# Transposes two groups ahead in a graph network's edge loop, with a new order of copy, softplus and bias

## The chip, the core and the metric

The kernel runs on one core of a Trainium2 chip, as one launch. The metric is the device time of a run in microseconds (us). The time before is the median of nine runs. One further execution was recorded by the hardware profiler; all durations below come from that one.

## What is computed

A layer of a graph network: 12500 nodes with 64 features, 200000 edges sorted by their destination, with 64 features each. Cut to what matters (`ssp(x) = softplus(x) - log 2`):

```python
nodes = node_state[edges].reshape(num_edges, -1)            # source and destination rows, 128 wide
gates = ssp(edge_state @ We1 + be1) @ We2 + be2
soft_cutoff = 1.0 - jax.nn.sigmoid(5.0 * (edges_distance - (CUTOFF - 1.5)))
gates = gates * soft_cutoff
h = ssp(nodes @ Wn1 + bn1) @ Wn2 + bn2
messages = h * gates
message_sum = jnp.zeros_like(node_state).at[edges[:, 1]].add(messages)
new_state = node_state + (ssp(message_sum @ Ws1 + bs1) @ Ws2 + bs2)
x = layernorm(x + new_state)
```

## The kernel before

The edges are cut into 391 groups of 512 (NG = 391, so `last` = 390). A group is four columns of 128 edges. For each group the kernel does the following, each on the engine named, in float32:

- **gather** (GpSimd, L233): an indirect DMA per column brings 128 rows of x, one per edge, into the tile `xg`. There are 19 buffers of `xg` (AHEAD + BEHIND), and the gathers of group i+14 are issued in step i. A few columns (26 in all) are not gathered but fetched as single rows by ScalarE's DMA queue into `xr` (`fetch`, L259, up to nine rows in a step). ROWS = (0, 9) gives the rows per step of SyncE's queue and of ScalarE's.
- **load** (SyncE, L280 and L288): the group's edge features `eT` and a window of 42 rows of a table that holds the destination's part of the first layer, into `wns`. Queued five steps ahead (LOADS).
- **onehot** (VectorE, L295): writes beside each gathered row which of 42 destinations of the window it belongs to. Both of its inputs are in SBUF.
- **transposes** (TensorE, L309; L306 for single rows): four transposes put features and one-hots on the partitions, in the PSUM tile `tx`, of which there are two buffers. Here the step waits for its gathers, loads and one-hot.
- **xcopy** (ScalarE, L316): `tx` to the SBUF tile `xT`.
- **layer 1** (TensorE): the bias (L321), the edge features (L326) and the node rows (L332) into the PSUM tile `z`, of which there are two buffers.
- **exps, logs** (ScalarE, L343 and L346) and **softplus** (VectorE, L351): the first nonlinearity, from `z` over `u` to `s`.
- **layer 2** (TensorE): the bias (L356), the gates (L363) and h (L368) into the PSUM tile `gh`.
- **hcut, message** (VectorE, L377 and L381): h times the cutoff, times the gates, to `msg`.
- **scatter** (TensorE, L385): `msg` times the one-hots, into a corner of the `z` tile of a later group.
- **window** (VectorE, L402): adds that corner to `sums` at the window's place.

In a step i of the loop TensorE works on layer 1 of group i+1, on layer 2 of group i and on an older group's scatter. `behind_by` says whose: group i-2 until the close, which begins at step 378 (`last - CLOSE`, CLOSE = 12); in step 378 both i-2 and i-1; after that i-1. The last two groups are written out behind the loop.

Whenever the groups that can reach a block of nodes are done, that block's own network and norm are put into the steps that follow (`node_block`, `parts`). Their TensorE parts (`hidden`, L421, and `layer2`, L449 and L452) use a `tx` tile and stand between `layer2(i)` and the end of the step. `hidden` reads `sums`, so it waits for the last window before it. In step 378 there is one such `hidden`.

The order of each engine's queue is the order of the program (`manual_schedule`): no scheduler moves anything. Each engine runs its queue in order, so what waits holds up what stands behind it on the same engine. GpSimd has only gathers in the loop.

Of the kernel before, what the change touches and what calls it, by code (L numbers as in the profile page):

```python
# [71 lines left out]
CLOSE = 12  # L72
# [53 lines left out]
def gnn_resnorm_kernel(ctx: ExitStack, tc: tile.TileContext, a: dict, out: bass.AP, E: int):  # L126
# [23 lines left out]
    def gh_tile():  # L150
        return psum.tile([P, NB], F32, name="gh")

    def tx_tile():
        return psum.tile([P, NB], F32, name="tx")
# [15 lines left out]
    packed, at = {}, 0  # L170
# [21 lines left out]
    def note(key, ins):  # L192
        made.setdefault(key, []).append(ins)
        return ins
# [19 lines left out]
    def arrived(g, k):  # L214
        n = by_rows[g, k]
        queue = slots[n][0]
        n -= firsts[queue]
        return landed[queue][n % LANDED], 16 * P * (n // LANDED + 1)
# [18 lines left out]
    def rows_left(queue):  # L237
        return (firsts[queue + 1] - firsts[queue]) * P - fetched[queue]
# [12 lines left out]
    def fetch(i, queue, count):  # L251

        for _ in range(min(count, rows_left(queue)) if i >= ROWS_FROM else 0):
            n, r = divmod(fetched[queue], P)
            n += firsts[queue]
            _, g, k = slots[n]
            if r == 0:
                row_tiles[n, "in"], xrs[g, k] = row_tile(queue, n), row_tile(queue, n)
            ins = queues[queue].dma_start(row_tiles[n, "in"][r : r + 1, :D].bitcast(U8),  # L259
                                          x_bytes[:, bass.ds(row_at[queue].pop(0), 4 * D)])  # L260
            tc.no_tile_sem_insts.add(ins.ins.name)
            ins.then_inc(arrived(g, k)[0], 16)
            if r == 0:
                behind(ins, ("rows read", n - 2))
            fetched[queue] += 1
# [3 lines left out]
    def row_tile(queue, n):  # L269
        return nc.alloc_sbuf_tensor_at(f"xr{queue}_{n % 2}", [P, P], F32,  # L270
                                       offset=rows_base + (2 * queue + n % 2) * 4 * P).ap()
# [30 lines left out]
    def transposes(g, *needs):  # L302
        tx = tx_tile()[:DW].rearrange("f (k e) -> f k e", k=K)
        for k in range(K):
            if (g, k) in by_rows:
                ins = nc.tensor.transpose(tx[:, k, :], xrs[g, k][:, :DW], ident)  # L306
                note(("rows read", by_rows[g, k]), ins.wait_op(*arrived(g, k), "sem-ge"))
            else:
                ins = nc.tensor.transpose(tx[:, k, :], xgs[g][:, k, :DW], ident)  # L309
            if k == 0:  # L310
                behind(ins, *needs)
        xTs[g] = tx

    def xcopy(g):
        xT = work.tile([DW, K, P], F32, name="xT", bufs=3)
        note(("xcopy", g), nc.scalar.copy(xT, xTs[g]))  # L316
        xTs[g] = xT.rearrange("f (t h) e -> f h t e", h=2)
# [17 lines left out]
    def z_of(g):  # L335
        return zs[g].rearrange("p b e -> p (b e)")[:, : 3 * HE]
# [11 lines left out]
    def softplus(g, part=every):  # L348
        if part.start == 0:
            ss[g] = work.tile([P, 3, 2, P], F32, name="s", bufs=3)  # L350
        nc.vector.scalar_tensor_tensor(ss[g].rearrange("p i t e -> p (i t e)")[:, part], us[g][:, part], BIG,  # L351
                                       z_of(g)[:, part], OP.min, OP.max)

    def layer2_bias(g):
        gh = gh_tile()
        nc.tensor.matmul(gh, ones3[:, :P], row3.rearrange("q i k d -> q (i k d)"), start=True, stop=False,  # L356
                         skip_group_check=True)
        ghs[g] = gh.rearrange("p (i k d) -> p i k d", i=2, k=K)
# [38 lines left out]
    def window(g):  # L397
        if g not in window_at:
            window_bases(g)
        for h in range(2):  # L400
            part = sums[h * D : (h + 1) * D, bass.ds(window_at[g][h], W)]
            nc.vector.tensor_add(part, part, scs[g][h * D : (h + 1) * D, h * W : (h + 1) * W])  # L402
# [89 lines left out]
    with tc.manual_schedule():  # L492
# [124 lines left out]
        with tc.tile_pool(name="finish", bufs=1) as finish:  # L617
            blocks = list(zip(node_blocks(N), block_steps(N, NG)))
            last = NG - 1
            parts, begun, complete, rest = {}, None, 0, []  # L620

            def at(f, g, *more):
                if 0 <= g < NG:
                    f(g, *more)

            def behind_by(i):
                close = last - CLOSE
                return [g for g in ([i - 2] if i <= close else []) + ([i - 1] if i >= close else []) if g >= 0]

            for g in range(LOADS - 1):  # L630
                load(g)
            for g in range(2):
                onehot(g)
            for i in range(-1, last - 1):
                now = parts.pop(i, [])
                early = [part for part in now if part.tensor]
                at(load, i + LOADS)
                if i >= 0:
                    at(gather, i + AHEAD)
                transposes(i + 1, ("load", i + 1), ("gather", i + 1), ("onehot", i + 1))  # L640
                xcopy(i + 1)
                read_rows(i, 1, ROWS[1])
                fetch(i, 1, ROWS[1] - 6)
                layer1_bias(i + 1)
                at(layer2_bias, i)
                for n, g in enumerate(behind_by(i)):
                    scatter(g, zs[i + 1][:, 1, HE + 2 * n * W : HE + 2 * (n + 1) * W])
                layer1_edge(i + 1)
                layer1_node(i + 1)
                exps(i + 1)  # L650
                fetch(i, 1, 3)
                logs(i + 1)
                fetch(i, 1, 3)
                for g in behind_by(i):
                    window(g)
                at(layer2, i)
                for part in early:
                    part.tensor(tx_tile())
                at(hcut, i)
                at(message, i)  # L660
                softplus(i + 1)
                for part in early:
                    part.others()
                at(onehot, i + 3)
                for part in now:
                    if not part.tensor:
                        part.others()
                complete = i
                if blocks and complete >= blocks[0][1] - PREPARE and not begun:
                    begun = node_block(*blocks[0][0], finish)  # L670
                    begun.pop(0).others()
                if blocks and complete >= blocks[0][1]:
                    steps = next(steps for steps in BLOCK_STEPS if i + steps[-1] < last - 1)
                    for n, part in zip(steps, begun):
                        parts.setdefault(i + n, []).append(part)
                    rest = begun[len(steps) :]
                    blocks.pop(0)
                    begun = None
            assert len(blocks) == 1 and begun and not parts


            begun.pop(2).others()
            transposes(last, ("load", last), ("gather", last), ("onehot", last))
            xcopy(last)
            layer1_bias(last)
            layer2_bias(last - 1)
            scatter(last - 2, zs[last][:, 1, HE : HE + 2 * W])
            layer1_edge(last)
            layer1_node(last)
            for some in (edge, node):  # L690
                exps(last, some)
                logs(last, some)
            square, variance, root, scale, store = (part.others for part in rest)
            square()
            window(last - 2)
            for g in range(last - 1, last + 1):
                window_bases(g)
            layer2(last - 1)
            layer2_bias(last)
            softplus(last, edge)  # L700
            layer2_edge(last)
            softplus(last, node)
            layer2_node(last)
            hcut(last - 1)
            message(last - 1)
            scatter(last - 1, tx_tile()[:, : 2 * W])
            variance()
            root()
            hcut(last)
            message(last)  # L710
            scatter(last, tx_tile()[:, : 2 * W])
            window(last - 1)
            window(last)
            hidden, clamp = begun.pop(0)
            hidden(gh_tile())
            scale()
            clamp()
            store()
            for part in begun:
                node_part(part)  # L720
# [154 lines left out]
```

## Time and profile before

| | before |
|---|---|
| median of 9 runs | 1960.89 us (1959.08 to 1963.64) |
| the profiled execution's own time | 1961.36 us |
| its span in the profile | 1959.4 us |
| TensorE matmuls (PE) | 1791.6 us busy, 91% of the span |
| TensorE weight loads (PEld) | 1467.0 us, 75% |
| VectorE (DVE) | 1048.8 us, 54% |
| ScalarE (ACT) | 964.4 us, 49% |
| GpSimd (POOL) | 1460.8 us, 75% |
| granted TensorE clock, mean | 0.971 |

A row of the groups shows line, engine, operation, output and inputs, and how often; then the busy time and the mean of one in ns; then the idle time of the engine just before these instructions and what ended most of it. A row of the timeline shows start and duration in us, and in square brackets the idle time before it and its releaser, where there was any. Matmuls are pipelined, so the busy time of one reaches into the next. A row of the chain of waits shows start and duration of the piece of work, or the wait, that set what came next. A row by stretches of time shows for each engine its busy time and number of instructions, in the order PE, PEld, DVE, ACT, POOL, and then the granted clock, the DMA share and GB/s.

### The profile page before, as it was taken

The numbers are of one execution on the slowest core, as the hardware profiler recorded it, in microseconds if no ns is written. First come the engines' busy times: TensorE is split into PE (matmuls) and PEld (weight loads), VectorE is DVE, ScalarE is ACT, GpSimd is POOL, SyncE is SP. The second block draws the span as 40 slices with busy tenths as digits, with TensorE's granted clock in tenths as the row PEclk, the third lists the DMA queues.
The fourth block names the chain that finished last, engine by engine and source line by source line (L and its number), as shares of the span: only waits on it lengthen the run. The fifth ranks groups of instructions, "written<-read, shape, count | busy, mean of one in ns | idle before, by whom it ended". The sixth has DMA issues, their size and how long they took to land.

```text
span 1959.4 us, 42161 instructions
## 1 busy us (share of the span) xinstructions
PE 1791.6 (91%) x11373; PEld 1467.0 (75%) x11373; DVE 1048.8 (54%) x2746; ACT 964.4 (49%) x1318; POOL 1460.8 (75%) x1541
## 2 busy tenths in 40 slices
PE   4899999999889989998989989998989999999997
PEld 4787777787777777777777777787777777777775
DVE  4355555555544545555555555555555555465555
ACT  1355555555444544444444444555455555455543
POOL 7777777777777777777777777777777777777773
PEclk9999999999999999999999998989999999899998
DMA  8423332332223232322232222332222232233221
GB/s 244 138 70 71 71 72 65 72 70 67 64 66 67 64 69 64 69 64 69 64 69 66 67 69 65 69 69 67 69 69 67 69 69 69 62 78 71 68 66 26
DMA packets 146162, 143.14 MB, mean 73 GB/s; under 512 B 46847, under 2 KB 93355, under 8 KB 145922
## 3 DMA queue, kind: packets, MB, share of 16 engines
q1 hardware_dynamic: 88714, 87.55, 15.5%
q0 software_dynamic: 49184, 50.46, 14.5%
q10 hardware_dynamic: 8024, 2.37, 0.6%
q8 instruction: 97, 1.59, 0.3%
q14 instruction: 143, 1.17, 0.2%
HBM read 130.58 MB, written 9.63 MB: 72 GB/s over the span
## 4 chain that ended last, share of the span: by engine, by line
PE 49%; ACTq 20%; issue 9%; ACT 8%; DMA 6%; DVE 4%; POOL 1%; SPq 1%; DVEq 0%; POOLq 0%
ACTq L259 17%; PE z L332 10%; PE gh L368 7%; PE z L385 7%; PE tx L309 7%; PE z L326 5%; ACT xT L316 4%; PE gh L363 4%; ACTq L247 3%; DMA xg<-in_x,src_i 3%; ACT u L343 3%; PE gh L356 2%; PE z L321 2%; DVE h L377 2%; PE z L593 2%
## 5 line engine op out<-in xcount | busy, mean ns | idle before, releaser
L233 POOL DMA_INDIRECT xg<-in_x,src_i x1537 | 1460.6, 950 | 471.4 <-issue 339.3
L343 ACT ACTIVATE u<-z 128x768 f32<-128x768 f32 x392 | 317.3, 809 | 703.5 <-PE z L332 687.7
L402 DVE TENSOR_TENSOR sums<-sums,z 64x42 f32 x778 | 152.9, 197 | 799.9 <-ACT u L343 770.9
L332 PE MATMUL z<-xT,wns 106*128 106x256 f32 x1564 | 427.3, 397 | 8.1 <-ACT xT L316 7.4
L368 PE MATMUL gh<-consts,s 128*128 128x64 f32 x3128 | 399.3, 271 | 0.0
L346 ACT ACTIVATE u<-u,one 128x768 f32<-128x768 f32 x392 | 366.0, 934 | 67.2 <-ACT u L343 64.2
L368 PEld LDWEIGHTS gh<-consts,s 128*128 128x128 f32 x3128 | 388.9, 195 | 0.1
L351 DVE SCALAR_TENSOR_TENSOR s<-u,z 128x768 f32<-128x768 f32 x392 | 369.2, 942 | 12.2 <-ACT u L346 10.0
L332 PEld LDWEIGHTS z<-xT,wns 106*128 106x128 f32 x1564 | 299.3, 197 | 78.1 <-ACT xT L316 31.4
L309 PE MATMUL tx<-consts,xg 128*106 128x128 f32 x1538 | 241.3, 278 | 111.5 <-DVE msg L381 31.5
L385 PEld LDWEIGHTS z<-xg,msg 128*128 128x128 f32 x1556 | 207.4, 194 | 127.2 <-issue 122.6
L316 ACT COPY xT<-tx 106x512 f32<-106x512 f32 x391 | 228.1, 583 | 147.0 <-PE tx L309 138.6
L309 PEld LDWEIGHTS tx<-consts,xg 128*106 128x106 f32 x1538 | 170.6, 139 | 133.4 <-issue 65.5
L385 PE MATMUL z<-xg,msg 128*128 128x84 f32 x1556 | 268.0, 295 | 1.2 <-DVE msg L381 0.6
L363 PEld LDWEIGHTS gh<-consts,s 128*128 128x128 f32 x1564 | 245.6, 198 | 25.2 <-DVE s L351 2.0
L326 PE MATMUL z<-eT,consts 128*128 128x256 f32 x782 | 256.9, 411 | 0.0
L363 PE MATMUL gh<-consts,s 128*128 128x128 f32 x1564 | 246.0, 280 | 1.7 <-DVE s L351 1.7
L377 DVE TENSOR_TENSOR h<-gh,cut 128x256 f32<-128x256 f32 x391 | 166.0, 424 | 31.6 <-PE gh L368 18.5
L381 DVE TENSOR_TENSOR msg<-gh,h 128x256 f32<-128x256 f32 x391 | 165.9, 424 | 13.4
L356 PE MATMUL gh<-row,ones 3*128 3x512 bf16 x391 | 148.4, 380 | 0.0
L295 DVE TENSOR_TENSOR xg<-consts,rel 128x168 f32<-128x168 f32 x391 | 128.3, 328 | 0.0
L326 PEld LDWEIGHTS z<-eT,consts 128*128 128x128 f32 x782 | 122.6, 198 | 1.2 <-issue 1.2
(93 smaller groups left out, 575.4 us busy)
## 6 DMA issues: line engine op xcount, KB each, us to landing
xr<-in_x ACTq DMA_DIRECT2D x3328, 0.2 KB
eT<-in_eT SPq DMA_DIRECT2D x195, 256.0 KB
xg<-in_x,src_i POOLq DMA_INDIRECT x1537
wns<-table SPq DMA_DIRECT2D x782, 21.0 KB
table<-tb SPq DMA_DIRECT2D x14, 448.0 KB
sums<-in_xT SPq DMA_DIRECT2D x7, 455.0 KB
y<-in_x SPq DMA_DIRECT2D x24, 128.0 KB
out<-y SPq DMA_DIRECT2D x24, 128.0 KB
```

What stands on the lines that cost most here:

```text
L233: note(("gather", g), nc.gpsimd.indirect_dma_start(out=xg[:, k, :D], out_offset=None, in_=x, in_offset=bass.IndirectOffsetOnAxis(ap=src_i[ ...
L259: ins = queues[queue].dma_start(row_tiles[n, "in"][r : r + 1, :D].bitcast(U8), x_bytes[:, bass.ds(row_at[queue].pop(0), 4 * D)])
L309: ins = nc.tensor.transpose(tx[:, k, :], xgs[g][:, k, :DW], ident)
L316: note(("xcopy", g), nc.scalar.copy(xT, xTs[g]))
L326: nc.tensor.matmul(zs[g][:, 0, :HE], we1.rearrange("a h d -> a (h d)"), eTs[g], start=False, stop=True, skip_group_check=True)
L332: nc.tensor.matmul(zn, wns[:, g % REST, h, :], xTs[g][:, h], start=True, stop=True, skip_group_check=True)
L343: nc.scalar.activation(us[g][:, part], z_of(g)[:, part], AF.Exp)
L346: nc.scalar.activation(us[g][:, part], us[g][:, part], AF.Ln, bias=one)
L351: nc.vector.scalar_tensor_tensor(ss[g].rearrange("p i t e -> p (i t e)")[:, part], us[g][:, part], BIG, z_of(g)[:, part], OP.min, OP.max)
L363: nc.tensor.matmul(v[:, 0, t], ss[g][:, 0, t, :], we2, start=False, stop=False, skip_group_check=True)
L368: nc.tensor.matmul(ghs[g][:, 1, 2 * t + h, :], ss[g][:, 1 + h, t, :], wn2, start=False, stop=h == 1 and t == 1, skip_group_check=True)
L385: ins = nc.tensor.matmul(sc, msgs[g][:, 2 * t : 2 * t + 2, :].rearrange("p h f -> p (h f)"), xgs[g][:, 2 * t : 2 * t + 2, D:DW], start=t = ...
```

## The change

The transposes run two groups ahead until the close: step i transposes group i+2 instead of i+1. Step -1 transposes groups 0 and 1, step 378 none, and the later steps i+1 as before. Until the close the copy of `tx` stands on ScalarE behind exps and logs of its step; the bias of layer 2 moves from the front of TensorE's step to just before layer 2; and softplus of group i+1 moves on VectorE ahead of `hcut` and `message` of group i. One-hots are made four groups ahead instead of three. Nothing is added to or taken from the work as a whole. In step 378 softplus already has its old place, and the bias still the new one.

```diff
+            def ahead_by(i):
+                return [0, 1] if i < 0 else [i + 2] if i < last - CLOSE else [i + 1] if i > last - CLOSE else []
+
             for g in range(LOADS - 1):
                 load(g)
-            for g in range(2):
+            for g in range(3):
                 onehot(g)
             for i in range(-1, last - 1):
...
-                transposes(i + 1, ("load", i + 1), ("gather", i + 1), ("onehot", i + 1))
-                xcopy(i + 1)
+                for g in ahead_by(i):
+                    transposes(g, ("load", g), ("gather", g), ("onehot", g))
+                    if i < 0 or i > last - CLOSE:
+                        xcopy(g)
                 read_rows(i, 1, ROWS[1])
                 fetch(i, 1, ROWS[1] - 6)
                 layer1_bias(i + 1)
-                at(layer2_bias, i)
+                if i > last - CLOSE:
+                    layer2_bias(i)
                 for n, g in enumerate(behind_by(i)):
                     scatter(g, zs[i + 1][:, 1, HE + 2 * n * W : HE + 2 * (n + 1) * W])
                 layer1_edge(i + 1)
...
                 logs(i + 1)
                 fetch(i, 1, 3)
+                if 0 <= i < last - CLOSE:
+                    xcopy(i + 2)
                 for g in behind_by(i):
                     window(g)
+                if 0 <= i <= last - CLOSE:
+                    layer2_bias(i)
                 at(layer2, i)
                 for part in early:
                     part.tensor(tx_tile())
+                if i < last - CLOSE:
+                    softplus(i + 1)
                 at(hcut, i)
                 at(message, i)
-                softplus(i + 1)
+                if i >= last - CLOSE:
+                    softplus(i + 1)
                 for part in early:
                     part.others()
-                at(onehot, i + 3)
+                at(onehot, i + 4)
```

## The prediction, made before the result was known

> **What bounds the kernel now.** I read the page's engine table and its group for the gathers first, then GpSimd alone near the end, then the chain of waits where the loop closes, then that place's timeline and clock.
>
> ```profile
> PE 1791.6 (91%) x11373; PEld 1467.0 (75%) x11373; DVE 1048.8 (54%) x2746; ACT 964.4 (49%) x1318; POOL 1460.8 (75%) x1541
> L233 POOL DMA_INDIRECT xg<-in_x,src_i x1537 | 1460.6, 950 | 471.4 <-issue 339.3
> ```
>
> TensorE shows 91%, but its group rows don't say whether it waits. GpSimd's row does: 1460.6 us busy and 471.4 idle over 1537 gathers is 0.307 us before each one. The timeline of GpSimd shows that this gap is always the same:
>
> ```profile
> 1927.68 1.07 POOL L233 DMA_INDIRECT xg<-in_x,src_i  x1 [0.30 <-issue]
> 1929.05 0.95 POOL L233 DMA_INDIRECT xg<-in_x,src_i  x1 [0.30 <-DMA xg<-in_x,src_i]
> 1930.30 0.94 POOL L233 DMA_INDIRECT xg<-in_x,src_i  x1 [0.30 <-DMA xg<-in_x,src_i]
> 1931.55 0.94 POOL L233 DMA_INDIRECT xg<-in_x,src_i  x1 [0.30 <-DMA xg<-in_x,src_i]
> ```
>
> A gather every 1.25 us, whoever is named as releaser: the gap belongs to the instruction, and GpSimd waited for nobody after its first index load (2.82 us). 1537 gathers from 3.29 to 1932.49 are 1929.2 us of the span of 1959.4. TensorE follows: from 600 to 1880 us a step takes 4.92 us (3.93 gathers), while steps that wait for nothing take 4.09 us (both from the starts of the transposes in the timeline). So some 0.83 us of a step is slack, and whatever the change saves or costs inside a steady step disappears in it. What can move the time is GpSimd's own row and the 27 us after its last gather. With last = 390 and CLOSE = 12 the close begins in step 378, and there TensorE stops waiting for gathers. The chain of waits:
>
> ```profile
> 1877.43 3.00 DMA xg<-in_x,src_i
> 1880.43 0.35 issue
> 1880.78 0.62 PE tx L309 x4
> 1881.40 0.21 PE z L321
> 1881.61 0.21 PE gh L356
> 1881.83 1.55 PE z L385 x8
> 1883.38 0.93 PE z L326 x2
> 1884.30 1.59 PE z L332 x4
> ```
>
> The transposes of group 379 are the last that a gather holds up; from 1880.78 to those of group 390 at 1934.69 the chain is TensorE, VectorE and ScalarE without a DMA. **After 1880.78 every piece of work added is added to the end.**
>
> **Part by part, without the close.** (1) A third one-hot ahead of the loop: 0.33 us of VectorE near 71.5 us, hidden by the wait of the first transposes (75.77) for a load of wns. (2) Transposes of group 1 in step -1: about 1.06 us of cold TensorE. First in danger is GpSimd, whose gather 19 reuses group 0's buffer and waits for its scatter: scatter(0) at 91.68, gather 19 at about 3.29 + 76 x 1.25 + 4.7 (the lengthened gathers of the prologue) = 103. Margin 11 us; cost 0. (3) Transposes a step earlier. They need SyncE's load of their group, queued five steps (24.6 us) ahead and now used after four; the first load took 2.3 us from issue (73.43) to the transposes it released. ScalarE's single rows are all issued by step g-7. Both stay early: 0. If that cover were gone, it would show as a DMA wait on SP's or ACT's names. (4) The copy behind exp and logarithm: ScalarE's cycle was log, three row DMAs, copy, three row DMAs, exp; it still is. What goes is TensorE's 7.4 us and PEld's 31.4 us of waiting for the copy, worth 0, because the next thing late is the gather. In the step after a node part the tx tile is released by that late copy, up to some 0.4 us late, under the 0.83. (5) The bias late: 0.21 us moved behind layer 1. (6) Softplus ahead: VectorE now waits for the logarithm before the cutoff's product, so h and msg of group i come 0.86 us plus that wait later; queued behind are msg and the one-hot. msg is read by a scatter two steps on (9.8 us): 0, except at the close. The first words of the change, single rows by ScalarE alone, have no line in the diff: ROWS is (0, 9) in both, and all 3328 xr DMAs are on ACTq already.
>
> (7) **The one-hot's instant.** Gathers longer than 0.95 us are not random:
>
> ```profile
> 1688.52 0.94 DVE L351 SCALAR_TENSOR_TENSOR s<-u,z 128x768 f32<-128x768 f32 x1
> 1689.38 0.33 DVE L295 TENSOR_TENSOR xg<-consts,rel 128x168 f32<-128x168 f32 x1
> 1689.45 1.08 POOL L233 DMA_INDIRECT xg<-in_x,src_i  x1 [0.30 <-issue]
> ```
>
> A one-hot that starts 0.03 to 0.2 us before a gather holds it until the one-hot is over. Of 260 one-hots from 600 to 1880 us, 21 start 1.05 to 1.22 us into GpSimd's 1.25 and 12 cost 0.115 us each: 1.4 us in all. A one-hot begins 5.97 us after its step's transposes (1875.08 to 1881.05). In the new order: transposes to exp 3.02 - 0.21 (bias gone), exp 0.84, log 0.98, softplus 0.86, h 0.46, msg 0.34 = 6.29, so 0.32 later. The one-hots then in danger are those that now lie at 0.74 to 0.91: 32. So 32/21 x 1.4 = 2.1 us: +0.7. Bounds: -1.4 (none hit), and +6 if a quarter of them fell there and all were held (65 x 0.115 = 7.5, less 1.4). I take +0.7, worked from where they lie now. The Trainium skill, GPSIMD Engine Reference, "8. Key points", says that VectorE instructions with two SBUF inputs contend with GpSimd for its SBUF interfaces; by the rule alone all 391 one-hots are exposed before and after alike, and this term would be 0.
>
> (8) **The close.** After the change group 379's transposes belong to step 377, which still has all its other work to do; before, they opened step 378. Both start at 1880.78. By the chain's durations: step 377 goes on with bias 0.21, scatter 0.60, edge 0.47, node 0.86 (to 1883.54), bias and layer 2 0.21 + 0.45 + 0.85 (to 1885.05). Step 378 has no transposes, but two scatters; the second needs msg(377), which now stands behind softplus(378): exp to 1884.38, log to 1885.36, softplus to 1886.22, h to 1886.68, msg to 1887.14. So TensorE waits from 1885.86 to 1887.14, then scatter 0.68, edge 0.47, node 0.86 (1889.15), exp 0.84, the two windows and their issue 1.48 (1886.76 to 1888.24 before): the node block's first product (L421), which needs window 377, starts at 1891.5. Before:
>
> ```profile
> 1886.76 0.42 DVE L402 TENSOR_TENSOR sums<-sums,z 64x42 f32 x2 [5.38 <-ACT u L343]
> 1887.68 0.42 DVE L402 TENSOR_TENSOR sums<-sums,z 64x42 f32 x2 [0.50 <-DVE sums L402]
> 1888.24 1.10 PE L421 MATMUL tx<-sums,consts 128*128 128x256 f32 x4 [1.08 <-DVE sums L402]
> ```
>
> That is +3.25 at full clock. But before ran part of this at half clock:
>
> ```profile
> 1880.00:1882.00 2.00, 1.22 (x8) 0.76 (x9) 1.38 (x3) 0.84 (x3) 1.69 (x2) 1.00 0.38 82
> 1882.00:1884.00 2.00, 2.00 (x10) 1.91 (x10) 0.00 (x0) 0.02 (x1) 1.39 (x3) 0.55 0.16 35
> 1884.00:1886.00 2.00, 2.00 (x8) 1.61 (x8) 0.00 (x0) 0.09 (x1) 1.64 (x2) 0.60 0.34 70
> ```
>
> The number after POOL's count is the granted clock: 1.00, 0.55, 0.60, after TensorE's idle 1.43 us in front of these transposes. The same wait remains, so I let the dip remain: two scatters, edge and node took 4.07 us instead of 2.6, so about 1.5 us more on the new chain: +4.7. Lower end 2.0 (no dip, and the second scatter not held, 1.28 less); upper end 7.0 (a second dip behind the new wait of 1.28 us: edge 0.46, node 0.73, L421 1.1). I take 4.7, nearest to the row at the same place. The Trainium skill, TensorE: Matmul & The Clock Gate, "Part 1", makes the clock fall after a whole idle window of about 3.4 us; neither wait is that long, and by the rule there is no dip after the change and the term is 3.25. From step 379 on the order is the old one, and before has no wait for a gather in it, so nothing is given back.
>
> **Sum.** The profiled execution took 1961.36 us (span 1959.4, 1.96 around it), 0.47 above the median of 1960.89. 1961.36 + 0.7 + 4.7 = 1966.8; against the median 1966.3, that is +0.28%. About 0.2% (3.9 us) is what a measurement of this kernel can tell from no change.
>
> **Rivals.** *A, the close absorbs it, so not slower.* TensorE's eleven steps from 379 take up the delay. Place: the transposes of group 390, now at 1934.69 with GpSimd's last gather begun at 1931.55, which by the 3.00 + 0.35 us of group 379 would release them at 1934.90. If TensorE caught up by then, the price is 0 to 2 us: 1960.9 to 1962.9. For it: the two are that close now. Against it: these steps take (1934.69 - 1889.18)/10 = 4.55 us with no DMA in the chain. It decides if most of the 4.7 can be made up where TensorE waits for msg now (0.43 and 0.22 us, timeline at 1908 and 1926); I see 0.65. A weaker form (no dip, no held scatter) ends at 1963 to 1964.5, still within 0.2%. Together 0.32. *B, one-hots locked onto the gather's start.* Steps follow the gathers, so their instants could settle in the bad 0.17 us: 260 x 0.115 = 30 us at worst, a third of it 10: 1972 to 1976. Against: the instants now spread over all of the 1.25. 0.05. *C, faster:* the 0.3 us gap is a wait after all, and TensorE's 0.83 us a step is to be had: 260 x 0.83 = 216 us, about 1745. Against: the gap is 0.30 to 0.32 in all 1536. 0.03.
>
> **Chances.** Forecast 0.60 (1964.9 to 1968.5), A 0.32, B 0.05, C 0.03. Slower by over 0.2%: 0.65; within: 0.32; faster: 0.03. The range must reach into A: 1961.8 to 1971.
>
> **What would show it.** Right: the gather row still 1537 with gaps of 0.30; the last gather's start within 2 us of 1931.55; a scatter (L385) waiting for msg just behind group 379's transposes; L421 3 to 5 us later there, and the transposes of group 390 as much later. L316's wait for L309 (138.6 us) nearly gone at no gain. Wrong: GpSimd gaps over 0.32, lengthened gathers by the dozen, or group 390's transposes at their old place.

## The result, and the profile after

| | before | after |
|---|---|---|
| median | 1960.87 us (32 runs, 1958.86 to 1963.64) | 1968.03 us (10 runs, 1964.81 to 1976.13) |
| ratio, 95% interval | | 1.0039 [1.0031, 1.0046] |
| profiled execution, span | 1961.36, 1959.4 us | 1973.53, 1971.4 us |
| granted TensorE clock, mean | 0.971 | 0.981 |

The change makes the kernel 7.2 us slower, against a forecast of 5.4. The profiled execution of after is a long one, 5.5 us above its own median, so its places are later than a typical run's. I read it for where time goes, and take sizes from the experiments.

First the engine table and the group of the gathers, from the page of after:

```profile
PE 1864.1 (95%) x11373; PEld 1447.3 (73%) x11373; DVE 1046.6 (53%) x2746; ACT 963.3 (49%) x1318; POOL 1461.7 (74%) x1541
L233 POOL DMA_INDIRECT xg<-in_x,src_i x1537 | 1461.5, 951 | 471.7 <-issue 337.4
```

GpSimd is as it was: 1537 gathers, 0.307 us idle before each. Its timeline at the end of after:

```profile
1931.51 0.94 POOL L233 DMA_INDIRECT xg<-in_x,src_i  x1 [0.30 <-DMA xg<-in_x,src_i]
1932.76 0.94 POOL L233 DMA_INDIRECT xg<-in_x,src_i  x1 [0.30 <-DMA xg<-in_x,src_i]
```

The last gather starts at 1932.76, before at 1931.55. So the gathers end 1.2 us later, in a span that is 12.0 longer; and at group 390 TensorE (1946.96) is 14.2 us behind the last gather, so it does not wait for it. PE shows 72.5 us more "busy" with the same work, which is no cost by itself: TensorE had slack in the steady steps. The loss is to be looked for in the close. The chain of waits of after (start, duration, what):

```profile
1884.58 0.44 PE tx L309 x4
1885.01 0.21 PE z L321
...
1887.20 0.82 ACT u L343
...
1889.02 0.95 DVE s L351
1889.97 0.34 DVE h L377
1890.34 0.43 DVE msg L381
...
1890.82 0.72 PE z L385 x4
1891.54 0.93 PE z L326 x2
1892.46 1.71 PE z L332 x4
```

Where before went straight from the bias of group 379 to eight scatter products, after goes through exp, logarithm, softplus, h and msg before the second scatter of step 378 can start. The same place in the timeline of after, with the wait in brackets and then the node block's first product:

```profile
1890.82 0.72 PE L385 MATMUL z<-xg,msg 128*128 128x84 f32 x4 [1.04 <-DVE msg L381]
...
1895.96 0.42 DVE L402 TENSOR_TENSOR sums<-sums,z 64x42 f32 x2 [0.49 <-DVE sums L402]
...
1897.25 2.02 PE L421 MATMUL tx<-sums,consts 128*128 128x256 f32 x4
```

And the stretches of after (the number after POOL's count is the granted clock):

```profile
1890.00:1892.00 2.00, 1.18 (x6) 1.10 (x7) 0.97 (x3) 0.00 (x0) 1.47 (x2) 0.83 0.22 45
1892.00:1894.00 2.00, 2.00 (x6) 1.17 (x4) 0.00 (x0) 0.00 (x0) 1.39 (x3) 0.50 0.35 54
...
1902.00:1904.00 2.00, 2.00 (x6) 1.55 (x6) 0.00 (x0) 0.00 (x0) 1.43 (x2) 0.50 0.16 29
1904.00:1906.00 2.00, 2.00 (x15) 1.91 (x14) 0.39 (x2) 1.35 (x2) 1.66 (x2) 0.76 0.26 54
```

Behind the wait for msg the clock is half for 13.7 us (1891.32 to 1904.97). Before's dip at the same stage was 3.4 us.

Rows I had not expected to change, the weight loads of layer 2's bias, of the gates and of the scatter, in the groups of before and then of after (busy, mean ns, idle in front):

```profile
L356 PEld LDWEIGHTS <-ones 3*128 3x128 bf16 x391 | 36.7, 94 | 0.1
L363 PEld LDWEIGHTS gh<-consts,s 128*128 128x128 f32 x1564 | 245.6, 198 | 25.2 <-DVE s L351 2.0
L385 PEld LDWEIGHTS z<-xg,msg 128*128 128x128 f32 x1556 | 207.4, 194 | 127.2 <-issue 122.6
```

```profile
L356 PEld LDWEIGHTS <-ones 3*128 3x128 bf16 x391 | 35.5, 91 | 128.1 <-issue 128.0
L363 PEld LDWEIGHTS gh<-consts,s 128*128 128x128 f32 x1564 | 207.6, 192 | 89.9 <-issue 76.5
L385 PEld LDWEIGHTS z<-xg,msg 128*128 128x128 f32 x1556 | 205.2, 192 | 52.1 <-DVE msg L381 4.8
```

In the old order the two bias products, the only bf16 ones of a step without a node part, stand side by side, with the scatter behind them. Apart, there is 0.33 us of idle in front of this bias's load and more in front of the gates' load behind it, and less in front of the scatter's: 128.0 + 64.7 - 75.1 = 117.6 us over the 391 groups. That the change of type makes the idle is not shown; no run has the bias in another type.

### The profile page after: what moved, and what is told of

Read it like the earlier page. It is cut to its first block, busy times and chain, and to the rows that moved or that the text cites. A ratio compares the mean times of both kernels' runs of the same rounds, so it can differ in the third digit from the quotient of the medians.

```text
span 1971.4 us, 42179 instructions
## 1 busy us (share of the span) xinstructions
PE 1864.1 (95%) x11373; PEld 1447.3 (73%) x11373; DVE 1046.6 (53%) x2746; ACT 963.3 (49%) x1318; POOL 1461.7 (74%) x1541
## 4 chain that ended last, share of the span: by engine, by line
PE 71%; DMA 8%; ACTq 7%; issue 5%; ACT 4%; DVE 2%; POOL 2%; DVEq 0%; SPq 0%; POOLq 0%
PE z L332 14%; PE gh L368 11%; PE z L385 10%; PE gh L363 9%; PE tx L309 8%; PE z L326 8%; DMA xg<-in_x,src_i 7%; ACTq L259 6%; PE gh L356 4%; PE z L321 3%; POOL xg L233 2%; PE z L593 2%; ACT xT L316 1%; ACT u L346 1%; DVE s L351 1%
## 5 line engine op out<-in xcount | busy, mean ns | idle before, releaser
L332 PE MATMUL z<-xT,wns 106*128 106x256 f32 x1564 | 410.7, 385 | 1.9 <-ACT xT L316 1.7
L346 ACT ACTIVATE u<-u,one 128x768 f32<-128x768 f32 x392 | 366.3, 934 | 67.0 <-ACT u L343 64.7
L368 PEld LDWEIGHTS gh<-consts,s 128*128 128x128 f32 x3128 | 385.8, 194 | 0.1
L309 PE MATMUL tx<-consts,xg 128*106 128x128 f32 x1538 | 242.2, 278 | 65.2 <-DMA xg<-in_x,src_i 25.7
L363 PE MATMUL gh<-consts,s 128*128 128x128 f32 x1564 | 280.5, 302 | 1.7 <-DVE s L351 1.7
L363 PEld LDWEIGHTS gh<-consts,s 128*128 128x128 f32 x1564 | 207.6, 192 | 89.9 <-issue 76.5
L326 PE MATMUL z<-eT,consts 128*128 128x256 f32 x782 | 252.0, 404 | 0.0
L316 ACT COPY xT<-tx 106x512 f32<-106x512 f32 x391 | 228.9, 586 | 29.0 <-PE tx L309 14.7
L309 PEld LDWEIGHTS tx<-consts,xg 128*106 128x106 f32 x1538 | 170.3, 140 | 88.4 <-PE gh L368 50.4
L356 PEld LDWEIGHTS <-ones 3*128 3x128 bf16 x391 | 35.5, 91 | 128.1 <-issue 128.0
## 6 DMA issues: line engine op xcount, KB each, us to landing
y<-in_x SPq DMA_DIRECT2D x24, 128.0 KB
out<-y SPq DMA_DIRECT2D x24, 128.0 KB
```

The costliest lines, as they stand in the source:

```text
L326: nc.tensor.matmul(zs[g][:, 0, :HE], we1.rearrange("a h d -> a (h d)"), eTs[g], start=False, stop=True, skip_group_check=True)
L332: nc.tensor.matmul(zn, wns[:, g % REST, h, :], xTs[g][:, h], start=True, stop=True, skip_group_check=True)
L346: nc.scalar.activation(us[g][:, part], us[g][:, part], AF.Ln, bias=one)
L363: nc.tensor.matmul(v[:, 0, t], ss[g][:, 0, t, :], we2, start=False, stop=False, skip_group_check=True)
L368: nc.tensor.matmul(ghs[g][:, 1, 2 * t + h, :], ss[g][:, 1 + h, t, :], wn2, start=False, stop=h == 1 and t == 1, skip_group_check=True)
```

## The experiments

*Theory 1:* the loss is made in steps 377 and 378, by a full step of work behind the last transposes that a gather holds up and by a scatter that waits for msg. *Theory 2:* the bias apart costs TensorE some 0.3 us a step, so it enters the close late and recovers slowly. *Rival:* the loss is made along the whole loop, by lengthened gathers. The runs came on three chips. On the one of the f runs the kernel before took 1960.9 us, as in the forecast; on those of the e, g and h runs it took 2573 to 2626 us, with waits between the gathers, so each run is compared with before on its own chip only. The bias late alone, the gathers left out and the added rows were not run on the chip of the f runs.

**Bias in front again** (e1, f1: the changed kernel with this alone undone):

```diff
-                if i > last - CLOSE:
-                    layer2_bias(i)
+                at(layer2_bias, i)
...
-                if 0 <= i <= last - CLOSE:
-                    layer2_bias(i)
```

> The changed kernel with one part undone: layer 2's bias stands at the front of TensorE's step everywhere, as before. Theory 1 (the whole loss is made in steps 377 and 378, where a full step of work follows the last transposes that a gather holds up, and a scatter waits for msg behind softplus): the bias plays no part, 1966 to 1968.5 us. Theory 2 (the bias apart from the other bias costs TensorE some 0.3 us in every step, 4.39 instead of 4.09 us, so it enters the close late and recovers slowly): about 2.4 us come back, 1964 to 1966, and the transposes of group 379 again start about 3.2 us after their last gather's start.

> The changed kernel with layer 2's bias at the front of TensorE's step everywhere, again, on a core whose transfers are not slowed. Theory 1 (the loss is made in steps 377 and 378 alone): 1966 to 1968.5 us. Theory 2 (the bias apart costs TensorE 0.3 us a step, and it enters the close late): 1964 to 1966. The runs on the slowed core speak for theory 2: there the kernel with the bias late alone was 10% slower than before, and this one was not.

f1: 1966.97 us, ratio 1.0032 [1.0020, 1.0044]: about 6.1 us of loss stay, so theory 2 is not the main cause. Its trace is the cleanest picture of the close, since TensorE is not late when it enters. The transposes of group 379 start at 1880.79, as before (1880.78). Its timeline from there:

```profile
1880.79 0.62 PE L309 MATMUL tx<-consts,xg 128*106 128x128 f32 x4 [0.35 <-PE gh L368]
...
1887.42 0.83 PE L385 MATMUL z<-xg,msg 128*128 128x84 f32 x4 [1.33 <-DVE msg L381]
...
1893.16 1.13 PE L421 MATMUL tx<-sums,consts 128*128 128x256 f32 x4 [0.77 <-DVE sums L402]
```

L421 is 4.92 us later than before (1888.24), and the transposes of group 390 are 4.78 later: the step that was forecast, alone. The span is 6.0 longer; the other 1.2 us arise behind group 390, where half clock begins 6.4 us after its transposes (1945.83), in before 9.0 (1943.64). e1, on a chip where GpSimd does not set the pace: 2605.57 us, ratio 0.9935 [0.9902, 0.9968]. There this order is a little faster than before.

**Bias late alone** (e4: the kernel before with only this part of the change):

```diff
-                at(layer2_bias, i)
+                if i > last - CLOSE:
+                    layer2_bias(i)
...
+                if 0 <= i <= last - CLOSE:
+                    layer2_bias(i)
```

> The kernel before with one part of the change alone: layer 2's bias just before layer 2, up to step 378. Theory 1: no change, 1960 to 1962. Theory 2: the step of TensorE that waits for nothing grows by 0.3 us, and the close starts late: 1962.5 to 1964.

2899.90 us, ratio 1.1035 [1.0966, 1.1104]. The price of the bias apart is plain in the shortest step between transposes, 600 to 1880 us. It is 4.09 us in before, f1, g3 and e1, where the two biases stand together; it is 4.39 in after, f2, g4 and e4, where they stand apart. So 0.30 us of TensorE a step, 117 us over 391 steps, where TensorE waits for nothing. That is not all of e4's 276 us: its clock is 0.727 on the mean, against 0.836 in e1, and how the rest divides is not shown.

**The old order from step 350 on** (e3, f3):

```diff
+BACK = 40
...
-                return [0, 1] if i < 0 else [i + 2] if i < last - CLOSE else [i + 1] if i > last - CLOSE else []
+                return [0, 1] if i < 0 else [i + 2] if i < last - BACK else [i + 1] if i > last - BACK else []
```

and BACK for CLOSE in the conditions of copy, bias and softplus.

> The changed kernel, but all of its parts go back to the old order at step 350 instead of 378; the scatter's own switch stays at 378. So TensorE has 28 steps in the old order, with some slack in each, to make up what the switch costs. Theory 1: nearly all of the loss comes back, 1960.5 to 1962.5. A rival, that the loss is made all along the loop (gathers held by one-hots, or a slower GpSimd): 26 of 28 parts of it stay, 1967 to 1968.

> The changed kernel with all parts going back to the old order at step 350 instead of 378, again. Theory 1 and theory 2 both: nearly all of the loss comes back, 1960.5 to 1962.5, since TensorE has 28 steps of the old order in which to catch up with the gathers. The rival that the loss is made all along the loop by longer gathers: 1967 to 1968.

f3: 1963.05 us, ratio 1.0008 [1.0000, 1.0017]. Some 5 of the 7.2 us return, so most of the loss is made at the close and not along the loop. The switch itself still costs: in f3 the transposes of group 351 start 9.22 us behind their last gather and those of 352, the first of the old order, 12.61 behind theirs. By group 374 that is down to 2.85, since here there is slack left in which to make it up. The timeline of f3 (its lines are one higher) shows the close:

```profile
1881.95 0.62 PE L310 MATMUL tx<-consts,xg 128*106 128x128 f32 x4 [1.47 <-DMA xg<-in_x,src_i]
...
1887.75 1.10 PE L422 MATMUL tx<-sums,consts 128*128 128x256 f32 x4 [1.08 <-DVE sums L403]
```

and its end, the last gather and the transposes of group 390:

```profile
1932.85 0.94 POOL L234 DMA_INDIRECT xg<-in_x,src_i  x1 [0.30 <-DMA xg<-in_x,src_i]
```

```profile
1936.01 0.60 PE L310 MATMUL tx<-consts,xg 128*106 128x128 f32 x4
```

3.16 us lie between them; in before it is 3.14 (1931.55, 1934.69). In f3 TensorE waits for gathers again in the close (0.30 us at group 385, for a gather's DMA), and the last gather is 1.30 us late, as late as the transposes of group 390 (1.32): that is most of the 2.1 that stay. e3: 2761.88 us, ratio 1.0477 [1.0405, 1.0550]. There the bias stays apart in 350 steps, and by e4 that weighs more than any close.

| start, us | before | after | f1, bias in front | f3, back at 350 |
|---|---|---|---|---|
| last gather | 1931.55 | 1932.76 | 1932.04 | 1932.85 |
| transposes of 379 | 1880.78 | 1884.41 | 1880.79 | 1881.95 |
| L421 (L422 in f3) | 1888.24 | 1897.25 | 1893.16 | 1887.75 |
| from transposes of 379 to L421 | 7.46 | 12.84 | 12.37 | 5.80 |
| transposes of 390 | 1934.69 | 1946.96 | 1939.47 | 1936.01 |
| span | 1959.4 | 1971.4 | 1965.4 | 1961.3 |

**Softplus in its old place** (e2, f2):

```diff
-                if i < last - CLOSE:
-                    softplus(i + 1)
                 at(hcut, i)
                 at(message, i)
-                if i >= last - CLOSE:
-                    softplus(i + 1)
+                softplus(i + 1)
```

> The changed kernel with one part undone: softplus of the next group stands behind the cutoff's product and the message everywhere, as before. Theory 1: the scatter of step 378 no longer waits for msg (1.04 us in the profile of the changed kernel, 1.3 in the forecast), 1966 to 1967. Theory 2: no change, 1967 to 1968.5.

> The changed kernel with softplus behind the message everywhere, again. Theory 1: the scatter of step 378 no longer waits for msg, 1966 to 1967. Theory 2: no change, 1967 to 1968.5.

A miss: f2 took 2128.72 us (2063 to 2170, too scattered for an interval), and e2 2814.36, ratio 1.0686 [1.0618, 1.0753]. The stretches of f2:

```profile
1745.00:1765.00 20.00, 19.30 (x69) 14.64 (x69) 5.21 (x14) 5.60 (x9) 7.55 (x8) 0.50 0.15 33
1765.00:1785.00 20.00, 20.00 (x71) 15.22 (x71) 6.97 (x17) 5.41 (x10) 8.18 (x9) 0.50 0.14 32
```

TensorE is back to back, at half clock, and GpSimd now waits for it (8 or 9 gathers in 20 us). At half clock a step takes 8.2 us, so it falls behind by 3.3 us a step. From 600 to 1880 us f2 runs 352 us at half clock, in stretches of up to 88.7 us; after has 44 in the same window, the longest 20.5, and before 96, the longest 13.7. So part of the change needs another part. Why the stretches last so long without the early softplus is not settled: f2's shortest step is after's 4.39 us.

What theory 1 said of the place does show in f2, where no half clock falls on it:

```profile
2043.89 0.60 PE L309 MATMUL tx<-consts,xg 128*106 128x128 f32 x4
...
2049.41 0.68 PE L385 MATMUL z<-xg,msg 128*128 128x84 f32 x4 [0.16 <-DVE msg L381]
...
2053.70 1.13 PE L421 MATMUL tx<-sums,consts 128*128 128x256 f32 x4 [0.48 <-DVE sums L402]
```

The wait for msg is nearly gone, and L421 starts 9.81 us after the transposes of 379. The next experiment has the same place with softplus ahead, also at full clock (g4): 10.99 us, with a wait of 1.04. The old order takes 5.80 there at full clock (f3). So the close's price is some 4.0 us for the full step behind the transposes (the bias apart is in it) and 1.2 for softplus ahead, and half clock comes on top. Before had half clock there, 7.46 us in all, so its loss in the close is less than the sum.

**Three gathers a group** (g3, g4: before and after without the gather of column 0, meant to let TensorE set the pace):

```diff
-            if (g, k) in by_rows:
+            if (g, k) in by_rows or k == 0:
...
-                ins = nc.tensor.transpose(tx[:, k, :], xgs[g][:, k, :DW], ident)
+                ins = nc.tensor.transpose(tx[:, k, :], xgs[g][:, max(k, 1), :DW], ident)
```

> The kernel before without the gather of column 0 (its transposes read column 1 instead), 1146 gathers: a step needs 3.67 us of GpSimd, so TensorE sets the pace. If GpSimd set it before: about 75 + 390 x 4.15 + 25 = 1720 us (between 1690 and 1760). If the step of 4.92 us is held by something else: no change from 1961.

> The changed kernel without the gather of column 0 (its transposes read column 1 instead), 1146 gathers, so that the new order's own price on TensorE shows. If the bias of layer 2 apart costs 0.3 us a step (4.39 against 4.09 us in the profiles' plain steps): 390 x 0.3 = 117 us slower than the kernel before with three gathers, about 1835. If what the new order saves TensorE (7.4 us of matmul waits and 31.4 us of weight-load waits for the copy) is what counts there: about 30 us faster than that one.

g3: 2045.20 us, ratio to before 0.7799 [0.7751, 0.7846]. g4: 2134.41, ratio 0.8098 [0.8039, 0.8157]. The absolute numbers were meant for the chip of the f runs, and TensorE did not set the pace alone: from 600 to 1880 us g3 takes 4.91 us a step, over its shortest 4.09. The difference is 89 us: of the sign of the 117 that the bias apart would make, and far from a gain of 30. It is no clean measure of the bias, since the clock differs too. By slices, from the page of g3 and then of g4 (its longest run, 2162.46 us):

```profile
PEclk9999999999999999999999999999999999999998
```

```profile
PEclk9977699958889999989789799999999999987998
```

The close of g4, from the transposes of group 379, at full clock:

```profile
2078.92 0.60 PE L309 MATMUL tx<-consts,xg 128*106 128x128 f32 x4
...
2085.32 0.68 PE L385 MATMUL z<-xg,msg 128*128 128x84 f32 x4 [1.04 <-DVE msg L381]
...
2089.91 1.13 PE L421 MATMUL tx<-sums,consts 128*128 128x256 f32 x4 [0.78 <-DVE sums L402]
```

**More single rows, fewer gathers** (g1: before with twelve rows a step on ScalarE; g2: the kernel of f3 with the same; h1: before with eight rows on SyncE beside ScalarE's nine):

```diff
-ROWS = (0, 9)
+ROWS = (0, 12)
```

```diff
-ROWS = (0, 9)
+ROWS = (8, 9)
...
+                read_rows(i, 0, ROWS[0])
+                fetch(i, 0, ROWS[0])
```

> The kernel before with ROWS = (0, 12) in place of (0, 9): 35 columns come as single rows by ScalarE's queue instead of 26, so there are 1528 gathers instead of 1537. If GpSimd's row sets the pace (the ground of the forecast), nine gathers at 1.25 us go: 1960.9 - 11.3 = 1949.6. ScalarE issues three more row DMAs behind its copy; at 0.36 us each (1.08 us for three in the timeline before) that is 1.08 us, of which 0.41 us fit in front of exp, so exp comes 0.67 us later in each step, still under TensorE's 0.83 us of slack. Rival: that eats the slack with the node parts' steps and the half clock, TensorE falls behind and the time goes up, by up to 260 x 0.2 = 50 us.

> The changed kernel with its old order from step 350 on (BACK = 40) and with ROWS = (0, 12): 1528 gathers. If GpSimd's row sets the pace: 1963.0 - 11.3 = 1951.7, the same gain as on the kernel before. If the new order is of use where ScalarE is the tight engine (the copy stands behind the logarithm, and TensorE does not wait for it), it gains here what the kernel before loses with twelve rows, and this version is the faster of the two. If the bias apart costs TensorE 0.3 us of its slack, it is the slower of the two.

> The kernel before with ROWS = (8, 9): SyncE fetches eight single rows at the front of each step, beside ScalarE's nine, so that 50 columns come as single rows instead of 26 and there are 1513 gathers instead of 1537. If GpSimd's row is what a step waits for: 24 gathers at 1.25 us go, 1960.9 - 30 = 1931; a step then has 3.87 gathers, 4.84 us, still over TensorE's 4.09, and the gap of 0.30 us stays. SyncE issues eight DMAs of some 0.35 us more in a step of 4.9 (2.8 us) and its loads, queued five steps ahead, stay early. If single rows on a second queue slow the transfers or hold up the loads, so that TensorE waits for them: gaps over 0.32 us in GpSimd's row and no gain, 1955 to 1985. Against the changed kernel at 1968.0 the forecast is 37 us less.

g1: 2659.42 us, 1.0108 [1.0057, 1.0158]. g2: 2741.73, 1.0331 [1.0244, 1.0417]. h1: 2639.77, 1.0255 [1.0217, 1.0293]. None gains, and none could show what it was made for: on this chip GpSimd does not set the pace. g2 is the slower of the first two, as was expected if the bias apart costs TensorE; its clock is lower as well (0.777 against 0.832). Timeline of h1, ScalarE's copy behind the logarithm's three row DMAs:

```profile
1303.66 0.58 ACT L316 COPY xT<-tx 106x512 f32<-106x512 f32 x1 [2.85 <-remote]
1303.99 0.94 POOL L233 DMA_INDIRECT xg<-in_x,src_i  x1 [1.53 <-DVE y L478]
```

The copy waits 2.85 us for something outside the core's engines, TensorE waits for the copy, and GpSimd's gap is 1.53 us here, and about that once a group. Whether fewer gathers beat both kernels where GpSimd sets the pace stays open; it was not tried there.

## Why the prediction was right, and what it missed

*The bound: right.* In after there are gaps of 0.30 to 0.32 us but for two near 18 us (0.36, 0.57), last gather 1.21 us later ("within 2 us").

*One-hots' instant, +0.7: right for the gathers, but not seen in the time.* From 600 to 1880 us, gathers that start within a one-hot and last over 0.99 us are 14 in before, 27 in after, 28 in f1 and 20 in f3; over 0.945 us they take 1.5, 2.4, 3.0 and 2.1 us in all, so +0.6 to +1.5. The last gather is 0.5 (f1) to 1.3 us (f3) later. The Trainium skill, GPSIMD Engine Reference, "8. Key points", exposes all one-hots to GpSimd alike and would have this term at 0; the measurement decides for the rows. But added to the close it was too much: in f1 the transposes of 379 start as in before, and at group 390 TensorE is 7.4 us behind the last gather (14.2 in after), so a late gather costs nothing there.

*The close, +4.7: right in place and mechanism, in size partly by luck.* f1 has it pure: +4.92 us at L421, a wait for msg of 1.33 us (1.28 forecast), and L421 at 1893.16 (1891.5 and 1.5 for the dip, 1893.0). The part at full clock is borne out: 10.7 us from the transposes of 379 to L421 were forecast, g4 takes 10.99. The 1.5 for the dip is luck. "The same wait remains" failed: f1 waits 0.35 us in front of those transposes, where before waited 1.43. A dip of before's length came all the same, but behind the new wait: in f1 from 1887.80 to 1891.21. In after it lasts 13.7 us; g4 has none behind a wait of 1.04, and f3 none behind one of 1.47. So in the profiled after L421 is 9.0 us later than before, outside the 3 to 5 named as a sign: 3.6 are TensorE's late entry, and the other 5.4 hold the longer dip. The Trainium skill, TensorE: Matmul & The Clock Gate, "Part 1", has the clock fall after a whole idle window of about 3.4 us; here it fell after a wait of 1.33 (f1) and of 1.04 (after), so the 3.25 by that rule was too little for f1's 4.92.

*The bias late, 0: wrong.* This is the step that failed. I priced the move by the 0.21 us that passes to another place, and not by its neighbour: taken apart from the other bias, it costs 0.30 us a step. It takes slack from 0.83 to about 0.5, so TensorE has less in which to catch up after a half-clock stretch. In the profiled after it was 5.57 us behind group 379's last gather, where before was 3.35 and f1 2.82. Undoing it alone gives back 1.1 us (7.2 to 6.1), which lies within the intervals. Where the 1.8 us lie that the forecast lacked is not shown; the sum also has no term for half clock behind group 390, which came sooner in f1's profiled run and went with 1.2 us there.

*"Nothing is given back": right in effect, for another reason.* Before does work off a delay in its close: its transposes are 6.68 us behind the gathers at group 380 and 2.84 at group 388. f1 goes from 11.17 to 6.79 over the same groups, 4.4 us to before's 3.8, and has 7.43 left at group 390. Neither waits for a gather from 380 to 390, and a step takes 4.55 us in before and 4.53 in f1. So rival A failed because what can be made up in the close was already used. Softplus ahead, priced at nothing until the close, is within this order no burden but a need there (f2).

*Rivals.* A (absorbed): the interval lies above 0.2%. B (locked one-hots): gathers 1.2 us later, not 10. C (the gap is a wait): gap unchanged. L316's wait for L309 fell from 138.6 to 14.7 us, at no gain, as forecast.

## What to carry to other kernels

When an instruction is moved, price what it leaves as well as where it goes: the two bias products cost 0.30 us a step less side by side than apart. In a loop bound by another engine, look where that engine lets go: a reordering that is nearly free in 377 steps showed its price in the step that changes back. And slack that looks unused is what works off a delay; spend it and the delay reaches the end.

## What the runs showed of the hardware

Half-clock stretches within the loop of before, after, f1, f2 and f3 come in lengths near multiples of 3.4 us (3.4, 6.8, 10.2, 13.7, 17.1, 20.5, 27.3, 37.5, 47.8, 88.7), start after some 0.8 to 2.2 us of TensorE idle time, and can outlast any idle: TensorE was busy 87.3 of the 89 us from 1725 to 1814 in f2, at 0.50. Before has 16 of them between 600 and 1880 us, mostly 3.4 long; after has 3, of 6.8 to 20.5. Not every such idle brings one (f3's 1.47 us at 1881.95 and g4's 1.04 at 2085.32 did not). What ends one, no run here shows. The kernel before took 1961 us on one chip and 2573 to 2626 on two others, where the bound was another, and an edit can change its sign there: the new order with the bias in front (f1, e1) is 0.3% slower than before on the first and 0.65% faster on one of the others.
